# Layer 0's two ends: the first keys' logarithms by products on TensorE, split weights, and the last projection spread between the last attention's steps

## The chip, the cores and the metric

The kernel runs on one NeuronCore of a Trainium2 chip. The metric is the device time of one execution in microseconds (us), lower is better. The profile is one execution recorded by the hardware profiler; its span is a little shorter than the time of the same execution as a run.

## The reference, cut to what matters

The network has four layers on x of shape (2, 512, 32, 32): a deformable attention with an MLP (layer 0), and three more attention layers. Only layer 0's attention is touched by the change. All arithmetic is in 32-bit floats.

```python
xn  = bn(x);  q = gconv1x1(xn, qw)                      # 8 groups of 64 channels
off = gelu(depthwise 6x6, stride 4, of q + dw_b)        # 8x8 places per group
off = tanh(off_pw_w . off) * 4                          # 64 sampling places, the keys
kv  = grid_sample(xn, places);  k, v = gconv1x1(kv, kw), gconv1x1(kv, vw)
pos = grid_q - grid_kv                                  # 1024 queries x 64 keys x (x, y)
bias = sign(pos) * log1p(abs(pos))
bias = relu(bias @ cpb_w1 + cpb_b1)                     # 2 -> 128
bias = relu(bias @ cpb_w2 + cpb_b2)                     # 128 -> 128
bias = bias @ cpb_w3 + cpb_b3                           # 128 -> 1
attn = softmax(q.k * scale + bias);  out = attn @ v
x = x + out_w @ out + out_b                             # the projection, then the MLP
```

The position `pos` separates into an x part and a y part, so for each key only 32 logarithms in x and 32 in y are needed. The first of the three small layers is a sum of an x table and a y table; the second (128 by 128, for each of 1024 queries and 64 keys, in 16 groups) is the bulk of layer 0's work.

## The kernel before, in words

The 512 channels lie in four tiles of 128 partitions (`CT`), for each of the two images (`B`). Two groups share a tile of 128 channels, so there are eight pairs (`BP`) and sixteen units `u`, one for each image and group.

**The front of a pair** (`offsets`, then `sampled`). `offsets` scales x to `xn` (L230), multiplies by the q weights (L237, `l0qkv[:, 0]`), copies q into a padded tile (L240), multiplies six rows of taps on DVE (`prod`, L244), reduces them (`conv`, L257), and then goes through gelu (L260), two tiny products (L265), tanh (L267), and the positions (L269 to L272) to `log`, the logarithms: 128 keys on the partitions, 32 in x and 32 in y on each (L280 to L284). It writes `log` to DRAM (`logs`, L286), and the places (`spots`, L288). `sampled` reads the places back, transposes `xn` (L305), builds bilinear weights `w` (L308 and after), sums `kv` by 32 records of products (L332: for each of the two halves of the channels, eight blocks of 128 pixels), and forms k and v (L345 to L353). Both are generators: the first pair's `offsets` runs straight through at the start, later ones go a step at a time between other work.

**The bias.** `table` loads 16 keys' logarithms, spread to all 128 partitions, from the DRAM copy by a DMA on SP's queue (L365: `lb`), makes the x table on POOL (`tx`, L367), and the y table on DVE into the PSUM tile `bank` (L379). `first_hidden` adds x and y tables and clips at zero by a custom DVE instruction (`h`, L391). `second_hidden` multiplies by `l0w2`, 32 hidden units at a time with four keys side by side (`hp`, L422), evicts on ACT (L427), and adds up the four parts by ACT, POOL and accumulating DMAs (L414 to L440). For the last block these sums are on DVE (L412, L440). `last_product` (L454) puts the sums into `sim` in PSUM. `l0w2` is `cpb_w2` times the magnitudes of `cpb_w3`; that multiplication (L183, L184, on `w3row`) is in `last_weights`.

**The attention** (`attend`) adds q·k to `sim` (L469), copies to `ss` (L477), transposes (L481), takes the softmax (L486 to L493), transposes back (L497, L501), multiplies by v (L506) and copies to `att` (L509). Its PSUM tiles come from the pool `ps`, three buffers of two banks, shared with `hp`. `project` and `project_one` multiply `att` by `ow` (L524) and add to x on DVE (L528): for each of four output tiles and two halves of the pixels, four products. The second image's projection comes after the last attention. Then `mlp0` loads its weights on SP's queue (L542), scales x on DVE (L550) and multiplies (L558, L567).

**What sets the order.** Layer 0 is inside `manual_schedule` for PE, ACT, DVE and POOL: these engines run in the order in which the code is written. The loop over `quads` (16 units, 8 blocks of keys, 2 halves) keeps `first_hidden` one quad ahead of `second_hidden`, and steps one generator of `front` and one of `after` at each quad. DMAs on SP's queue, and the work of `mlp0`, are placed by the framework. The first loads are issued on ACT's queue in this order: `cols`, `grid`, `l0_qkv` (768 KB), `cpb_w2`, `out_w`, `cpb_w3`; x goes on SP's.

Of the kernel before, what the change touches and what calls it, by code (L numbers as in the profile page):

```python
# [18 lines left out]
P = 128  # L19
# [28 lines left out]
class Net:  # L48
# [16 lines left out]
    def prologue(self, ctx: ExitStack):  # L65
        nc, io = self.nc, self.io
        const = self.const = self.pool(ctx, "const")
        xpool = self.pool(ctx, "x")
        self.cols = const.tile([P, NCOL], F32, tag="cols", name="cols")
        nc.scalar.dma_start(self.cols, io["cols"])  # L70
        self.grid = const.tile([P, NGRID], F32, tag="grid", name="grid")
        nc.scalar.dma_start(self.grid, io["grid"])
# [26 lines left out]
    def layer0(self):  # L99
# [3 lines left out]
        with ExitStack() as ctx:  # L103
            keep = self.pool(ctx, "l0")
            self.l0qkv = keep.tile([P, 3, CT, P], F32, tag="qkv", name="qkv")
            nc.scalar.dma_start(self.l0qkv, io["l0_qkv"])
            self.l0w2 = keep.tile([P, P], F32, tag="w2", name="w2")
            nc.scalar.dma_start(self.l0w2, io["cpb_w2"])
            ow = keep.tile([P, CT, C], F32, tag="ow", name="ow")
            nc.scalar.dma_start(ow, io["out_w"])  # L110
            self.s1 = self.bn(keep, "bn1")
            self.last_weights(keep)
# [62 lines left out]
    def last_weights(self, keep):  # L175

# [1 line left out]


        nc = self.nc  # L180
        row = keep.tile([P, P], F32, tag="row", name="w3row")
        nc.scalar.dma_start(row, self.io["cpb_w3"].partition_broadcast(P))
        nc.vector.scalar_tensor_tensor(row, row, -1.0, row, ALU.mult, ALU.max)  # L183
        nc.vector.tensor_tensor(self.l0w2, self.l0w2, row, ALU.mult)  # L184
# [11 lines left out]
        for k in range(4):  # L196
            rows = slice(32 * k, 32 * k + 32)
            nc.vector.tensor_copy(self.ends[rows, 28 + k : 29 + k], sign[rows, 3:4])

    @staticmethod  # L200
    def step(behind):
# [21 lines left out]
    def offsets(self, m, bt, ps):  # L223
# [65 lines left out]
        m["logs"], m["spots"] = logs, spots  # L289
        yield  # L290

    def sampled(self, m, bt, ps):
# [33 lines left out]
        nc.vector.scalar_tensor_tensor(w, w, 0.0, wx.unsqueeze(1).to_broadcast([P, NB, 2 * NJ]), ALU.max, ALU.mult)  # L326
        yield
        kv_ps = self.bank[:, 384:448]
        for par in range(2):
            rows = slice(par * DH, (par + 1) * DH)  # L330
            for n in range(NB):
                nc.tensor.matmul(  # L332
                    kv_ps[rows, :],
                    lhsT=xnT[:, n, rows],
                    rhs=w[:, n, rows],
                    start=(n == 0),
                    stop=(n == NB - 1),
                )
# [18 lines left out]
    def table(self, u, o, pairs, tables):  # L357
# [9 lines left out]
            nc.gpsimd.tensor_scalar(x, got[:, :, :, 0, :], self.col("cpb_w1", 0), self.col("cpb_b1"), ALU.mult, ALU.add)  # L367
            tables["next"] = got, x

        if o % 2 == 0:  # L370
            if u == o == 0:
                load(0, 0)
            tables["logs"], tables["x"] = tables.pop("next")
        elif u < 2 * BP - 1 or o < 7:

            load(*((u, o // 2 + 1) if o < 7 else (u + 1, 0)))
        y = self.bank[:, 0:256].rearrange("p (j i x) -> p j i x", j=2, i=4)
        i = 4 * (o % 2)
        nc.vector.tensor_scalar(y, tables["logs"][:, :, i : i + 4, 1, :], self.col("cpb_w1", 1), None, ALU.mult)  # L379
# [82 lines left out]
    def attend(self, u, m, sim, att, ps):  # L462
# [16 lines left out]
        tp = ps.tile([P, 8, NJ], F32, tag="ps", name=f"tp{u}")  # L479
# [12 lines left out]
        nc.vector.reciprocal(st[:, 2, :], st[:, 1, :])  # L492
        nc.vector.tensor_tensor(e, e, st[:, 2, :].unsqueeze(2).to_broadcast([P, 8, NJ]), ALU.mult)  # L493
        yield
        pp = ps.tile([P, HF], F32, tag="ps", name=f"pp{u}")
        for i in range(4):
            nc.tensor.transpose(  # L497
                pp[:, i * P : (i + 1) * P], e[:, 2 * i : 2 * i + 2, :].rearrange("p a j -> p (a j)"), self.ident
# [1 line left out]
        pt = self.soft.tile([P, HF], F32, tag="pt", name=f"pt{u}")  # L500
        nc.vector.tensor_copy(pt, pp)  # L501
        yield
        o = ps.tile([P, N], F32, tag="ps", name=f"o{u}")
        for h in range(2):
            half = slice(h * NJ, (h + 1) * NJ)
            nc.tensor.matmul(  # L506
                o[rows, h * HF : (h + 1) * HF], lhsT=m["v"][half, rows], rhs=pt[half, :], start=True, stop=True
            )
        nc.scalar.copy(att[g // 2][rows, :], o[rows, :])  # L509
        yield  # L510

    def project(self, ps, att, w, bias: str, b: int):
# [652 lines left out]
```

## Time and profile before

| | |
|---|---|
| three timed runs | 3599.56, 3600.17, 3602.11 us; median 3600.17 |
| profiled execution | 3599.09 us as a run, span 3597.3 us |
| mean TensorE clock granted | 0.989 |
| PE busy, 0 to 42 us | 3.85 us |
| PE busy, 42 to 60 us | 17.76 of 18 us |
| PE busy, 60 to 2080 us (layer 0's loop) | 2007.84 of 2020 us |
| PE busy, 2080 to 2100 us (last attention) | 11.04 of 20 us |
| PE busy, 2100 to 2130 us (last projection) | 29.11 of 30 us |
| PE busy, 2130 to 3597 us (MLP, layers 1 to 3) | 1430.98 of 1467 us |

PE is TensorE's multiplication, PEld its weight loads, DVE is VectorE, ACT is ScalarE, POOL is GpSimd, SP the queue of SyncE. A 32-bit product is recorded as two rows ("x2" for one matmul). In the page, a group is line, engine, operation, output and inputs, count, then busy time and mean duration; behind the next bar stand the idle time of the engine just before and what ended it. In a timeline, a row is start, busy time, engine, line, what, and in brackets the idle time before. In the chain of waits, a row is start, length and what the end of the program waited for.

### The profile page before, as it was taken

Reading aid. Unit: us, or ns where it says so; the run is one execution under the profiler, and the core shown is the slowest. Engines: PE = TensorE matmul, PEld = TensorE weight load, DVE = VectorE, ACT = ScalarE, POOL = GpSimd, SP = SyncE. Lnnn points to the kernel's source line nnn. Section 1 sums busy time; section 2 is a strip of 40 time slices with the busy share of each in tenths; the row PEclk is TensorE's granted clock in tenths of the full one; section 3 lists DMA queues with packets and bytes.
Section 4 is the critical chain, followed back from the end, with each engine's and each line's share of the span. In section 5 each row is a group of like instructions: output and inputs, shape, how many; then the busy total and the mean of one; then the engine's idle time right before and its main releaser. Section 6 shows DMA issues by size and latency. Waiting matters only on the chain.

```text
span 3597.3 us, 58774 instructions
## 1 busy us (share of the span) xinstructions
PE 3500.6 (97%) x25152; PEld 1249.1 (35%) x25152; DVE 2019.9 (56%) x2074; ACT 1974.7 (55%) x2001; POOL 1871.8 (52%) x1393
## 2 busy tenths in 40 slices
PE   5999999999999999999999989999999999999999
PEld 2333332332333332332333334444644333443333
DVE  5767767767767668768666620000242476423664
ACT  4877777787776677777777720111010465102661
POOL 3878787787786687787788810000011344012441
PEclk8999999999999999999999999999999999999999
DMA  5878777787786687787788740000000000000001
GB/s 144 157 138 158 149 154 144 151 161 146 152 160 125 122 161 143 149 160 147 165 163 161 147 159 0 0 0 0 1 3 0 36 1 2 15 0 1 1 1 48
DMA packets 101924, 335.20 MB, mean 93 GB/s; under 512 B 12560, under 2 KB 14224, under 8 KB 100368
## 3 DMA queue, kind: packets, MB, share of 16 engines
q0 software_dynamic: 73296, 266.90, 39.2%
q1 hardware_dynamic: 27488, 62.34, 5.9%
q8 instruction: 201, 3.29, 0.4%
q10 hardware_dynamic: 864, 2.06, 0.2%
q14 instruction: 75, 0.61, 0.1%
HBM read 59.92 MB, written 4.46 MB: 18 GB/s over the span
## 4 chain that ended last, share of the span: by engine, by line
PE 93%; DVE 5%; DMA 1%; issue 0%; ACT 0%; POOL 0%; ACTq 0%; SPq 0%; DVEq 0%; POOLq 0%
PE hp L422 47%; PE m L558 6%; PE m L567 6%; PE o L924 6%; PE s L895 6%; PE pb L524 3%; PE qk0p L787 3%; PE qk1p L787 3%; PE sim L454 3%; PE vp L828 3%; PE out_b L524 2%; DVE h L391 2%; DVE prod L244 1%; PE d L941 1%; DVE conv L257 1%
## 5 line engine op out<-in xcount | busy, mean ns | idle before, releaser
L422 PE MATMUL hp<-h,w 128*32 128x512 f32 x16384 | 1823.4, 593 | 17.7 <-DVE h L391 16.2
L391 DVE CUSTOM_DVE_ANT_1 h<-tx,bank 128x1024 f32<-128x1024 f32 x1024 | 1181.0, 1216 | 345.0 <-PE hp L422 321.9
L427 ACT ACTIVATE h<-hp,magb 128x1024 f32<-128x1024 f32 x1024 | 1123.6, 1112 | 451.5 <-PE hp L422 450.6
L422 PEld LDWEIGHTS hp<-h,w 128*32 128x32 f32 x16384 | 528.9, 110 | 1242.3 <-issue 1152.5
L414 POOL DMA_DIRECT2D h<-h x509 | 452.3, 1026 | 377.1 <-ACT h L433 319.9
L440 POOL TENSOR_TENSOR h<-h,h 128x1024 f32<-128x1024 f32 x255 | 614.7, 2410 | 21.3
L438 POOL TENSOR_SCALAR h<-h,flip 128x1024 f32<-128x1024 f32 x256 | 449.0, 1754 | 0.9 <-ACT h L427 0.9
L899 ACT ACTIVATE e<-s 128x1024 f32<-128x1024 f32 x256 | 258.6, 1024 | 153.4 <-PE s L895 153.3
L429 ACT ACTIVATE h<-h,flip 128x1024 f32<-128x1024 f32 x256 | 291.3, 1138 | 0.0
L895 PE MATMUL s<-q,k 64*64 64x512 f32 x2048 | 260.0, 590 | 5.4 <-ACT e L899 3.7
L924 PE MATMUL o<-e,v 64*64 64x512 f32 x2048 | 260.8, 592 | 0.1
L598 POOL MEMSET l1ones<- 128x128 f32 x1 | 0.2, 205 | 486.4 <-PE m L567 486.4
L562 ACT ACTIVATE mh<-m,cols 128x512 f32<-128x512 f32 x64 | 44.0, 687 | 336.5 <-PE m L558 336.5
L558 PE MATMUL m<-mx,w 128*128 128x512 f32 x512 | 220.5, 592 | 0.9 <-issue 0.9
L567 PE MATMUL m<-mh,w 128*128 128x512 f32 x512 | 220.4, 592 | 0.0
L906 POOL TENSOR_TENSOR some<-some,e 128x1024 f32<-128x1024 f32 x64 | 151.4, 2365 | 82.5 <-ACT e L899 80.1
L575 DVE SCALAR_TENSOR_TENSOR x<-m,cols,x 128x512 f32<-128x512 f32 x16 | 12.0, 751 | 318.0 <-PE m L567 318.0
L431 POOL TENSOR_SCALAR h<-h,flip 128x1024 f32<-128x1024 f32 x128 | 156.0, 1219 | 64.5 <-ACT h L427 63.6
L904 POOL TENSOR_TENSOR some<-e,e 128x1024 f32<-128x1024 f32 x32 | 75.9, 2371 | 213.3 <-ACT q L933 129.2
L801 POOL TENSOR_TENSOR sq<-q 128x1024 f32<-128x1024 f32 x16 | 30.3, 1895 | 280.0 <-DVE q L795 280.0
L799 ACT ACTIVATE k<-qk1p,cols 128x512 f32<-128x512 f32 x32 | 22.0, 688 | 243.5 <-PE qk1p L787 243.5
L433 ACT ACTIVATE h<-h,flip 128x1024 f32<-128x1024 f32 x128 | 145.6, 1138 | 0.0
(185 smaller groups left out, 2710.5 us busy)
## 6 DMA issues: line engine op xcount, KB each, us to landing
h<-h POOLq DMA_DIRECT2D x509, 512.0 KB, 6.5
lb<-logs SPq DMA_DIRECT2D x64, 512.0 KB, 5.3
w<-in_mlp_w SPq DMA_DIRECT2D x8, 1024.0 KB, 12.0
qkv<-in_l_qkv SPq DMA_DIRECT2D x8, 768.0 KB, 6.4
x<-in_x SPq DMA_DIRECT2D x8, 512.0 KB, 7.8
out<-x SPq DMA_DIRECT2D x8, 512.0 KB, 2.6
proj<-in_l_proj SPq DMA_DIRECT2D x8, 256.0 KB, 5.9
l1w<-in_l_w SPq DMA_DIRECT2D x1, 1280.0 KB, 8.7
```

Of the source, the lines that this page charges most:

```text
L391: self.nc.vector._custom_dve(TENSOR_ADD_SAT, out=h[:, k, :, :], in0=x[:, jj, 2 * r + k, :].unsqueeze(1).to_broadcast([P, H, W]), in1=y[:, ...
L414: nc.gpsimd.dma_start(to, what, accum_op=ALU.add)
L422: nc.tensor.matmul(hp[rows, cut], lhsT=self.l0w2[:, 32 * q : 32 * q + 32], rhs=h1[k][:, cut], start=True, stop=True)
L427: nc.scalar.activation(y, hp, AF.Relu, bias=self.magb[:, q : q + 1])
L429: nc.scalar.activation(ys[0], ys[0], AF.Copy, scale=self.flip[:, 0:1])
L438: nc.gpsimd.tensor_scalar(y, y, self.flip[:, 2:3], 1.0, ALU.mult, ALU.mult)
L440: (nc.vector if final else nc.gpsimd).tensor_tensor(y, y, ys[2], ALU.add)
L558: nc.tensor.matmul(acc, lhsT=w1[t][:, o * P : (o + 1) * P], rhs=xn[t], start=(t == 0), stop=(t == CT - 1))
L567: nc.tensor.matmul(acc, lhsT=w2[t // 4][:, t % 4, o * P : (o + 1) * P], rhs=hs[t], start=(t == 0), stop=(t == nh - 1),)
L895: nc.tensor.matmul(s[halves[c], par, :], lhsT=ks[p][rows, at : at + DH], rhs=qs[p][rows, cut], start=True, stop=True)
L899: nc.scalar.activation(e, s, AF.Exp)
L924: nc.tensor.matmul(o[halves[par], r, :], lhsT=v[rows, n, at : at + DH], rhs=e[rows, par, :], start=(n == 0), stop=(n == NB - 1),)
```

## The change

1. The first load. `l0_qkv` is split: the q third (256 KB) goes second on ACT's queue, ahead of `grid`; the k and v thirds go after `cpb_w2` and `cpb_w3`, ahead of `out_w`.
2. `fold_weights`: the two DVE instructions that multiply `l0w2` by `w3row` move behind the first pair's `conv`.
3. The first 16 keys' logarithms are no longer loaded from DRAM. Sixteen products with a column of the identity matrix, repeated 128 times as weights, spread a row of `log` over all partitions into a PSUM tile (`lb_ps`). ACT makes the x table from it and copies it to `lb`; DVE takes the first y table from PSUM, the second from the copy. POOL's first `tx` and SP's first `lb` load are gone.
4. In `sampled`, the loops over channel halves (`par`) and pixel blocks (`n`) change places.
5. The end. `held` has the last two blocks' sums. The new generator `share` keeps three output tiles of the last projection in the three buffers of `ps`, and adds the products of one `att` tile at a time: `att[0]` between the two `last_product` calls, `att[1]` after the q·k step, `att[2]` after the softmax's first step, `att[3]`, with the additions to x, at the end. The last `attend` uses `bank` and `sim` for its PSUM tiles, and its last copy is split between ACT and DVE. The fourth output tile is projected last, as before.

```diff
-            nc.scalar.dma_start(self.l0qkv, io["l0_qkv"])
+            nc.scalar.dma_start(self.l0qkv[:, 0], io["l0_qkv"][:, 0])
+            nc.scalar.dma_start(self.grid, io["grid"])
...
+            nc.scalar.dma_start(self.l0qkv[:, 1:3], io["l0_qkv"][:, 1:3])
...
-                for _ in self.offsets(pairs[0], 0, ps):
-                    pass
+                for n, _ in enumerate(self.offsets(pairs[0], 0, ps)):
+                    if n == 4:
+                        self.fold_weights()
...
-                for done in held:
-                    self.last_product(*done, sims, ps_s)
-                after.append(self.attend(u, pairs[u // 2], sims.pop(u), att, ps))
                 self.advance(after, lambda: False)
-                self.project(ps, att, ow, "out_b", B - 1)
+                self.last_product(*held[0], sims, ps_s)
+                accs = [ps.tile([P, 2, HF], F32, tag="ps", name=f"ob{o}") for o in range(CT - 1)]
+                share = self.share(accs, att, ow)
+                next(share)
+                self.last_product(*held[1], sims, ps_s)
+                for n, _ in enumerate(self.attend(u, pairs[u // 2], sims.pop(u), att, None)):
+                    if n in (0, 1):
+                        next(share)
+                for _ in share:
+                    pass
+                for h in range(2):
+                    self.project_one(ps, att, ow, "out_b", B - 1, CT - 1, h)
+
+    def share(self, accs, att, w):
+        nc = self.nc
+        for t in range(CT):
+            for o, acc in enumerate(accs):
+                for h in range(2):
+                    nc.tensor.matmul(
+                        acc[:, h, :],
+                        lhsT=w[:, t, o * P : (o + 1) * P],
+                        rhs=att[t][:, h * HF : (h + 1) * HF],
+                        start=(t == 0),
+                        stop=(t == CT - 1),
+                    )
+                    if t == CT - 1:
+                        xt = self.xs[B - 1][o][:, h * HF : (h + 1) * HF]
+                        nc.vector.scalar_tensor_tensor(xt, acc[:, h, :], self.col("out_b", o), xt, ALU.add, ALU.add)
+            if t < CT - 1:
+                yield
...
-        for par in range(2):
-            rows = slice(par * DH, (par + 1) * DH)
-            for n in range(NB):
+        for n in range(NB):
+            for par in range(2):
+                rows = slice(par * DH, (par + 1) * DH)
...
+        if u == o == 0:
+            logs = self.ps_h.tile([P, 2, 8, 2, W], F32, tag="ps", name="lb_ps")
+            for j in range(2):
+                for k in range(8):
+                    key = j * 32 + k
+                    nc.tensor.matmul(
+                        logs[:, j, k, :, :].rearrange("p d x -> p (d x)"),
+                        lhsT=self.ident[:, key : key + 1].to_broadcast([P, P]),
+                        rhs=pairs[0]["log"].rearrange("p d x -> p (d x)"),
+                        start=True,
+                        stop=True,
+                    )
+            x = self.tab.tile([P, 2, 8, W], F32, tag="x", name="tx00")
+            nc.scalar.activation(
+                x, logs[:, :, :, 0, :], AF.Identity, scale=self.col("cpb_w1", 0), bias=self.col("cpb_b1")
+            )
+            got = self.lpool.tile([P, 2, 8, 2, W], F32, tag="logs", name="lb00")
+            nc.scalar.copy(got, logs)
+            tables["logs"], tables["x"], tables["rest"] = logs, x, got
...
-        o = ps.tile([P, N], F32, tag="ps", name=f"o{u}")
-        for h in range(2):
+        if ps:
+            o = ps.tile([P, N], F32, tag="ps", name=f"o{u}")
+            parts = [o[:, h * HF : (h + 1) * HF] for h in range(2)]
+        else:
+            parts = [self.bank, sim]
+        for h, part in enumerate(parts):
             half = slice(h * NJ, (h + 1) * NJ)
...
+        else:
+            nc.scalar.copy(to[rows, 0:HF], self.bank[rows, :])
+            nc.vector.tensor_copy(to[rows, HF:N], sim[rows, :])
```

More of the change, by code (lines that the diff above doesn't have):

```diff
@@ L71, in prologue @@
         self.grid = const.tile([P, NGRID], F32, tag="grid", name="grid")
-        nc.scalar.dma_start(self.grid, io["grid"])
         x_in = io["x"].rearrange("b (t p) h w -> b t p (h w)", p=P)
@@ L105, in layer0 @@
             self.l0qkv = keep.tile([P, 3, CT, P], F32, tag="qkv", name="qkv")
-            nc.scalar.dma_start(self.l0qkv, io["l0_qkv"])
+            nc.scalar.dma_start(self.l0qkv[:, 0], io["l0_qkv"][:, 0])
+            nc.scalar.dma_start(self.grid, io["grid"])
             self.l0w2 = keep.tile([P, P], F32, tag="w2", name="w2")
             nc.scalar.dma_start(self.l0w2, io["cpb_w2"])
+            self.s1 = self.bn(keep, "bn1")
+            self.last_weights(keep)
+            nc.scalar.dma_start(self.l0qkv[:, 1:3], io["l0_qkv"][:, 1:3])
             ow = keep.tile([P, CT, C], F32, tag="ow", name="ow")
             nc.scalar.dma_start(ow, io["out_w"])
-            self.s1 = self.bn(keep, "bn1")
-            self.last_weights(keep)
             self.dram = ctx.enter_context(self.tc.tile_pool(name="l0_d", bufs=2, space=bass.MemoryType.DRAM))
@@ L168, in layer0 @@
                 self.join(True)
-                for done in held:
-                    self.last_product(*done, sims, ps_s)
-                after.append(self.attend(u, pairs[u // 2], sims.pop(u), att, ps))
                 self.advance(after, lambda: False)
-                self.project(ps, att, ow, "out_b", B - 1)
+                self.last_product(*held[0], sims, ps_s)
[27 more added lines that the diff above has]
+                yield
     def last_weights(self, keep):
         nc = self.nc
[L181 to L184, printed above, removed]
+        self.w3row = keep.tile([P, P], F32, tag="row", name="w3row")
+        nc.scalar.dma_start(self.w3row, self.io["cpb_w3"].partition_broadcast(P))
         w3 = self.colr("w3r", 4)
@@ L198, in last_weights, with fold_weights @@
             nc.vector.tensor_copy(self.ends[rows, 28 + k : 29 + k], sign[rows, 3:4])
+    def fold_weights(self):
+        nc, row = self.nc, self.w3row
+        nc.vector.scalar_tensor_tensor(row, row, -1.0, row, ALU.mult, ALU.max)
+        nc.vector.tensor_tensor(self.l0w2, self.l0w2, row, ALU.mult)
     @staticmethod
@@ L288, in offsets @@
         nc.sync.dma_start(spots, at)
-        m["logs"], m["spots"] = logs, spots
+        m["log"], m["logs"], m["spots"] = log, logs, spots
         yield
@@ L368, in load @@
             tables["next"] = got, x
-        if o % 2 == 0:
-            if u == o == 0:
-                load(0, 0)
+        if u == o == 0:
[17 more added lines that the diff above has]
+            tables["logs"], tables["x"], tables["rest"] = logs, x, got
+        elif o % 2 == 0:
             tables["logs"], tables["x"] = tables.pop("next")
@@ L376, in table @@
             load(*((u, o // 2 + 1) if o < 7 else (u + 1, 0)))
+        if u == 0 and o == 1:
+            tables["logs"] = tables.pop("rest")
         y = self.bank[:, 0:256].rearrange("p (j i x) -> p j i x", j=2, i=4)
@@ L478, in attend @@
         yield
-        tp = ps.tile([P, 8, NJ], F32, tag="ps", name=f"tp{u}")
+        tp = ps.tile([P, 8, NJ], F32, tag="ps", name=f"tp{u}") if ps else self.bank.rearrange("p (a j) -> p a j", j=NJ)
         for i in range(4):
@@ L494, in attend @@
         yield
-        pp = ps.tile([P, HF], F32, tag="ps", name=f"pp{u}")
+        pp = ps.tile([P, HF], F32, tag="ps", name=f"pp{u}") if ps else self.bank
         for i in range(4):
@@ L502, in attend @@
         yield
-        o = ps.tile([P, N], F32, tag="ps", name=f"o{u}")
-        for h in range(2):
-            half = slice(h * NJ, (h + 1) * NJ)
[L506 to L509, printed above, removed]
+        if ps:
[4 more added lines that the diff above has]
+        for h, part in enumerate(parts):
+            half = slice(h * NJ, (h + 1) * NJ)
+            nc.tensor.matmul(part[rows, :], lhsT=m["v"][half, rows], rhs=pt[half, :], start=True, stop=True)
+        to = att[g // 2]
+        if ps:
+            nc.scalar.copy(to[rows, :], o[rows, :])
+        else:
+            nc.scalar.copy(to[rows, 0:HF], self.bank[rows, :])
+            nc.vector.tensor_copy(to[rows, HF:N], sim[rows, :])
         yield
```

## The prediction

> **What bounds the kernel now.** I read the page first: engine shares, then the 40 slices. TensorE is the bound almost everywhere; only a few slices show it idle, and the change touches two of them: the first slice, and the one around 2090 us that hides the end of layer 0.
>
> ```profile
> PE 3500.6 (97%) x25152; PEld 1249.1 (35%) x25152; DVE 2019.9 (56%) x2074; ACT 1974.7 (55%) x2001; POOL 1871.8 (52%) x1393
> ...
> PE   5999999999999999999999989999999999999999
> ```
>
> A microsecond saved where PE is full, or on a chain that PE waits for, is a microsecond of span; elsewhere nothing. So next the chain of waits over the first 60 us (start, length, what):
>
> ```profile
> 1.18 5.12 DMA grid<-in_grid
> 6.32 10.98 DMA w3row<-in_cpb_w
> 17.32 0.30 DVE w3row L183
> 17.64 0.04 DVE w L184
> 17.86 4.54 DVE prod L244 x6
> 22.42 4.01 DVE conv L257
> 31.11 3.74 DMA logs<-log
> 34.87 5.11 DMA lb<-logs
> 40.16 0.78 POOL tx L367
> 40.97 1.23 DVE h L391
> ```
>
> Until 42.24, when the first `hp` product starts, everything is latency. Two waits stand out: DVE is held for `w3row` until 17.3, though `qpad` was ready at 14.40; and `log`, finished at 30.37, goes to DRAM and back before the tables exist at about 40.0. The timeline adds the first product, held by its weights:
>
> ```profile
> 9.87 3.47 PE L237 MATMUL q<-xn,qkv 128*128 128x512 f32 x4 [9.87 <-DMA qkv<-in_l_qkv]
> ```
>
> `xn` ended at 6.99, so PE waited 2.9 us for the 768 KB load alone. The windows give PE 2007.84 busy of the 2020 us from 60 to 2080, so an earlier start is kept. Then the timeline at layer 0's end:
>
> ```profile
> 2084.80 1.07 PE L454 MATMUL sim<-h,ends 128*32 128x512 f32 x3 [2.38 <-DVE h L412]
> 2094.72 1.09 PE L497 MATMUL pp<-ident,e 128*128 128x128 f32 x4 [4.73 <-DVE e L493]
> 2098.59 29.36 PE L524 MATMUL out_b<-att,ow 128*128 128x512 f32 x64
> 2103.95 0.75 DVE L528 SCALAR_TENSOR_TENSOR x<-out_b,cols,x 128x512 f32<-128x512 f32 x1 [7.41 <-PE out_b L524]
> 2128.83 16.55 PE L558 MATMUL m<-mx,w 128*128 128x512 f32 x38 [0.89 <-issue]
> ```
>
> From about 2082 to 2098.6 PE has only the last attention's short products between DVE and ACT steps; then 64 records of projection, the first four at half speed, then the MLP. Last, groups by shape on PE (busy us, mean ns), for a part that the change's title does not name:
>
> ```profile
> L332 PE MATMUL bank<-w,xnT 128*64 128x64 f32 x256 | 16.6, 237 | 2.8 <-DVE h L391 2.8
> L661 PE MATMUL m<-kn,xT 128*128 128x65 f32 x128 | 14.6, 275 | 0.0
> ```
>
> **What the Trainium skill says.** "TensorE: Matmul & The Clock Gate", Part 1: PE runs at half clock after an idle window and at full clock after about 3.4 us of activity. The trace agrees: records start 0.86 us apart from 2098.6 to about 2101.7, 0.43 after; at 42 us the switch took about 4.7. The same page, "LDWEIGHTS (loading the stationary operand)": a load takes its columns over 1.2 GHz, 53 ns for 64. The trace agrees: 32 records of L332 take 1.76 us of loads, 55 ns each. "TensorEngine Tiling (Array Packing)", "Key Properties": different tiles can load and multiply in parallel. `hp` agrees: four 32-column loads of 0.11 us each together take 0.13. "PSUM — Partial Sum Buffer", the section on bank collisions: two engines must not touch one bank and quadrant at once, two reads included. The trace has such a wait: ACT's copy of `v` (L353) starts 0.03 after DVE's (L352) ends, both reading one `bank`.
>
> **The change, part by part.**
>
> *First weights.* The q third of `l0_qkv` (256 KB) is issued second on ACT's queue, ahead of `grid`; 768 KB landed at 9.8, having moved at some 219 KB/us (half of the 425 GB/s that the DMA view shows, the x loads taking the rest). 512 KB less is 2.3 us: landing 7.4, bounds 7.0 (then `xn` binds) and 8.6 (smaller packets, smaller share). Gain 2.4, from 1.3 to 2.9. The issues behind it (`grid`, w2, `w3row`, the other two thirds, `ow`, which now waits for x00 at about 6.2) leave ACT's queue by about 7, and its table load still ends before q's copy is due near 11. `grid`, w2 and `w3row` go early and small; they are needed from about 20. Two thirds of qkv and `ow` are needed only after 80 us.
>
> *The fold.* L183 and L184 go behind the reduce. DVE no longer waits 17.86 − 14.40 = 3.45 us; the 0.58 us of the two instructions lies under ge, its product and tanh (26.42 to 27.48, 1.06 us). Gain 3.45. Bounds 2.9 to 3.5.
>
> *Logs by products.* `log` would then end at 30.37 − 2.4 − 3.45 = 24.5. SP's DRAM write and the reload for later keys stay, off the path; one `lb` load leaves SP's queue, POOL's first tx (0.77) its own; the second `lb` load follows the DRAM write at about 29 and lands near 35, two table halves before its use. In their place: 16 products of 128x64, 32 records each with a 128-column load. L661 has just this form: 14.6/128 = 0.114 us each, load-bound, so 3.7 us at full clock, 7.3 at half. PE is cold; with 3.9 us at half clock (the middle of 3.1 and 4.7; about 17 records) and 15 after, 5.6 us, tail 0.3. Then ACT: tx from PSUM, 0.69 (as L562), the copy to `lb`, 1.02 (as L240), and only then DVE's y, 0.49: the built program has y wait for that copy, the collision rule. Hand-overs 0.2. So h begins at 24.5 + 5.9 + 0.7 + 1.0 + 0.5 + 0.2 = 32.8 instead of 40.97: 8.2 us for the three parts together. PE being warmed already may give 0.3 more (the first eviction came 2.64 us after the last h, about 2.0 when warm). Start: 8.5, bounds 6 (all cold, weights late) and 10.
>
> *kv products.* L332's two halves alternate now, so neighbours use different 64-column tiles. Each of 8 groups holds PE 1.82 us (82.80 to 84.62). If pairs run together, 16 × 0.055 + 0.15 = 1.05: 0.77 saved, 6 us over 8 groups; PE is full around them, ACT idles 2.8 us just after. No row shows two alternating 64-column tiles at K = 128, so the bounds are 0 and 7; I take 6, since `hp` alternates tiles at full overlap. The loss side is a rival below.
>
> *The end.* In before's clock. PE finishes the earlier held products' records near 2081.7 and starts six projection products (12 records, 5.15 us) on att0; the three PSUM buffers are free at 2081.14. Ends 2087.0. Then the last `sim` products and q·k, warm, 8 + 8 records four abreast: 1.7, to 2088.9. They were ready at 2084.8: the attention's chain is put back, and with it bn2s on DVE (queued ahead of ss), and SP's eight MLP loads, by 1.3 us. ss ends about 2090.1, hidden under att1's six products (to 2094.2), as are six mx on DVE. Transposes to 2094.9; max, subtract, exp, sum, reciprocal, multiply (0.68 + 0.69 + 0.63 + 0.68 + 0.19 + 0.69, hand-overs) to 2098.6, under att2's six (to 2099.8). Then bare again: pp, pt, o, copies to att3: to 2103.0. Last six on att3: the built program makes each second half wait for the DVE add of the first half of the same tile. Per tile: product to end 1.02, add 0.75, hand-overs 0.1, second half 0.86: 2.73, thrice 8.2, not 5.15. To 2111.2. Eight products of the fourth tile, 16 × 0.43 = 6.9, to 2118.0; drain, add: the MLP starts 2119.1 instead of 2128.83. Gain 9.8, bounds 8 (more drains between tile shapes) and 11.5 (no stall at the halves). The MLP's weights landed by about 2108; 1.3 later still leaves 9 us.
>
> Sum: 8.5 + 6 + 9.8 = 24.3 us against the profiled span 3597.3, which was 3599.09 as a run; the three timed runs lie from 3599.56 to 3602.11. From their median: 3600.17 − 24.3 = 3575.9.
>
> **Rivals.**
> 1. The alternation gives nothing, loads in both tiles sharing one path: 18.3 us, 3581.9. For: 55 ns is exactly one load's time. Against: four `hp` loads overlap. Chance 0.25.
> 2. One of the ends gives little: PE stays cold through the logs' products and the weights come late, and the share's inserted work drains PE at each change of shape: 6 + 8, with alternation 0 to 6: 14 to 20, so 3580 to 3586. Chance 0.12.
> 3. Slower: alternating 64-column tiles in L332 drains the array each time. A record then costs its latency, 0.222 us instead of 0.057: 32 × 0.222 − 1.82 = 5.3 more per group, 42 over 8, minus 18.3: 24 later, 3624. It cancels the rest from 0.071 us more per record. Against: `hp` changes tile at every record at 0.107. Chance 0.03.
> 4. The program doesn't do what it says: the end bound by something else (weights, a DVE queue), the start's gain lost again before 60 us: within 7 us of before. Chance 0.04.
> The likeliest, at 0.56, is the sum.
>
> **How the numbers follow.** 0.2% is 7.2 us, about what a measurement can tell from no change. Faster by over that: 0.56 + 0.25 + 0.12 = 0.93; same 0.04; slower 0.03. Range: best bounds 10 + 7 + 11.5 = 28.5 give 3571.7, the spread of runs 1 more: 3571; the upper end takes in rivals 1 and 2: 3587.
>
> **What would show it.** Right: `q` starts near 7.4, `prod` directly after q's copy, `lb_ps` 32 records in some 5.6 us, h before 33.5; L332 busy about 8 to 9 us instead of 16.6; MLP's first product 9 to 10 us earlier relative to the last `hp`; DVE adds between the halves in the att3 step. Wrong: PE waiting for `mlp_w` at the MLP's start; PE idle growing in 60 to 2080; L332 unchanged or longer; `hp` starting after 36.

## The result, and the profile after

The changed kernel takes 3578.0 us (median of six runs, 3576.96 to 3579.59) against 3601.1 (six runs beside them, 3597.06 to 3602.11): ratio 0.9938, interval 0.9925 to 0.9951. The forecast was 3575.9 in a range from 3571 to 3587. The profiled span falls from 3597.3 to 3576.3 us, by 21.0, where the sum said 24.3.

On the page, PE has almost the same busy time in a shorter span, the first slice is fuller, and the notch around 2090 us has closed:

```profile
PE 3497.6 (98%) x25184; PEld 1248.3 (35%) x25184; DVE 2023.0 (57%) x2075; ACT 1976.3 (55%) x2003; POOL 1869.8 (52%) x1392
...
PE   7999999999999999999999999999999999999998
```

The chain of waits at the start (start, length, what). Neither `w3row` nor a transfer of `log` stands in it any more:

```profile
6.04 0.82 DVE xn L264
...
6.91 3.79 PE q L271 x4
...
11.85 4.54 DVE prod L278 x6
...
24.14 0.24 DVE log L318
...
24.51 7.08 PE lb_ps L410 x32
...
32.39 0.91 ACT lb L422
...
33.33 0.50 DVE bank L433
33.85 1.23 DVE h L445
```

`q` no longer waits for its weights but for `xn`; `prod` begins 6.0 us earlier than before (11.85, not 17.86); the longest piece is now the 32 records of `lb_ps`. Between `lb` and `bank` is the wait that the prediction named: DVE's y table follows ACT's copy.

The kv products, a group by shape (busy us, mean ns, then the idle time before), formerly 16.6 and 237:

```profile
L366 PE MATMUL bank<-w,xnT 128*64 128x64 f32 x256 | 9.5, 229 | 2.8 <-DVE h L445 2.8
```

A single record is as long as before, but neighbours overlap: in seven of the eight groups 32 records take 1.15 us from the first start to the last end, formerly 1.90. And the end, in PE's timeline: the `att[3]` step with DVE additions between its halves, the fourth tile, the MLP:

```profile
2090.68 1.13 PE L193 MATMUL ob<-att,ow 128*128 128x512 f32 x2 [0.66 <-ACT att L569]
2092.65 1.98 PE L193 MATMUL ob<-att,ow 128*128 128x512 f32 x4 [0.84 <-DVE x L202]
...
2099.27 7.03 PE L585 MATMUL out_b<-att,ow 128*128 128x512 f32 x16
2107.19 1.10 PE L619 MATMUL m<-mx,w 128*128 128x512 f32 x2 [0.89 <-issue]
```

To see where the 21.0 us come from, I followed the same instruction through both timelines and took the difference of its starts, the lead:

| at | before, us | after, us | lead |
|---|---|---|---|
| first eviction of `hp` | 48.27 | 41.29 | 6.98 |
| last quad's `hp` | 2072.91 | 2061.67 | 11.24 |
| MLP's first product | 2128.83 | 2107.19 | 21.64 |
| end of the span | 3597.3 | 3576.3 | 21.0 |

In the loop the lead rises by some 0.75 us at each of the groups of kv products (0.5 at the second), about 5.8 in all, and it falls twice by about 0.8, near 612 and near 1116 us: 6.98 + 5.8 − 1.6 is 11.2. Both falls come at a front whose second step of three `prod` takes 6.06 us on DVE in the changed kernel and 5.28 in the kernel before. Below, the first is called the long way and the second the short way of this step. After the MLP's start 0.6 is lost again; nothing of the change lies there.

### The profile page after: what moved, and what is told of

Its sections match the earlier page's. It is cut to its first block, busy times and chain, and to the rows that moved or that the text cites. A ratio compares the mean times of both kernels' runs of the same rounds, so it can differ in the third digit from the quotient of the medians.

```text
span 3576.3 us, 58840 instructions
## 1 busy us (share of the span) xinstructions
PE 3497.6 (98%) x25184; PEld 1248.3 (35%) x25184; DVE 2023.0 (57%) x2075; ACT 1976.3 (55%) x2003; POOL 1869.8 (52%) x1392
## 4 chain that ended last, share of the span: by engine, by line
PE 94%; DVE 5%; issue 1%; ACT 0%; POOL 0%; DMA 0%; DVEq 0%; ACTq 0%
PE hp L476 47%; PE m L619 6%; PE m L628 6%; PE s L956 6%; PE o L985 6%; PE qk0p L848 3%; PE pb L585 3%; PE qk1p L848 3%; PE sim L508 3%; PE vp L889 3%; DVE h L445 2%; DVE prod L278 1%; PE out_b L585 1%; PE d L1002 1%; DVE conv L291 1%; PE ob L193 1%
## 5 line engine op out<-in xcount | busy, mean ns | idle before, releaser
L960 ACT ACTIVATE e<-s 128x1024 f32<-128x1024 f32 x256 | 258.7, 1024 | 152.7 <-PE s L956 152.6
```

The source lines that it names most:

```text
L960: nc.scalar.activation(e, s, AF.Exp)
```

## The experiments

Each kernel is the changed one with the edit shown, except where it says otherwise, and the times of before beside them were medians of 3600.0 to 3602.7 us. In the runs with extra products (e5, e8, e11, e12) nothing is left out; the extra results are read by nobody. What is compared is mostly a stretch of the profile. Each kernel left one profile, and its span also holds the losses of 0.8 us, whose number differs from one profile to the next.

**e1: the kv loops put back.**

```diff
-        for n in range(NB):
-            for par in range(2):
-                rows = slice(par * DH, (par + 1) * DH)
+        for par in range(2):
+            rows = slice(par * DH, (par + 1) * DH)
+            for n in range(NB):
```

> The changed kernel with the loops over channel halves and pixel blocks in the kv products put back. Theory (alternating 64-column tiles overlap, PE is the bound): the kv group is busy 16.6 us again instead of 9.5; each of the eight groups costs 0.75 us more, 6 us in all, and the two places where the changed kernel lost 0.8 us on DVE (near 612 and 1107 us in its trace) may fall either way: span 3576.3 + 4 to 6 = 3580 to 3582. Rival (the gain lies in the ends alone): within 1 us of 3576.3.

Measured: 3585.11 us, ratio 0.9952 (0.9935 to 0.9969), span 3579.6. The group is back where it was, with the alternation as the only difference:

```profile
L366 PE MATMUL bank<-w,xnT 128*64 128x64 f32 x256 | 16.6, 236 | 2.8 <-DVE h L445 2.8
```

The last `hp` starts at 2066.46 instead of 2061.67, 4.8 us later; with one more front that went the short way here (three, against two), that is 5.6 for the eight groups. The alternation is what saves the time in that group, and rivals 1 and 3 of the prediction are out.

**e2: the first keys from DRAM again.**

```diff
-        if u == o == 0:
-            logs = self.ps_h.tile([P, 2, 8, 2, W], F32, tag="ps", name="lb_ps")
...
-        elif o % 2 == 0:
+        if o % 2 == 0:
+            if u == o == 0:
+                load(0, 0)
...
```

> The changed kernel with the first 16 keys' logarithms loaded from DRAM again. Theory A (the products were worth little because PE was cold through all 32 records, 7.06 us): log still ends at 24.4, the reload takes the 10.6 us that it took in the kernel before, h starts at 35.0 instead of 33.85, span about 1.1 us longer, 3577.4. Rival B (the products made most of the start's 7 us): h near 39, span 3581.

Measured: 3581.03 us, ratio 0.9940 (0.9923 to 0.9956), span 3579.1. DVE's timeline, where h waits for the x table on POOL again:

```profile
35.67 9.14 DVE L425 CUSTOM_DVE_ANT_1 h<-tx,bank 128x1024 f32<-128x1024 f32 x8 [0.40 <-POOL tx L401]
```

`log` ends at 24.66 and h starts at 35.67, 11.0 us later. With the products it was 24.37 and 33.85, 9.5 us. The products are worth 1.5 us at h (1.9 at the first eviction, 43.52 against 41.29, less the 0.3 by which `log` was late), and not the 2.3 that their part of the sum contains (10.6 of before, from 30.37 to 40.97, less 8.3): the 7.06 us of `lb_ps` take most of what the two transfers took.

**e3: the end put back.** `share` is not used, and `attend` and `project` stand as before.

```diff
...
-                self.last_product(*held[0], sims, ps_s)
-                accs = [ps.tile([P, 2, HF], F32, tag="ps", name=f"ob{o}") for o in range(CT - 1)]
-                share = self.share(accs, att, ow)
...
+                self.project(ps, att, ow, "out_b", B - 1)
```

> The changed kernel with the end of layer 0 as it was: no share, the whole projection after the last attention. Theory: from the start of the last quad's hp to the MLP's first product 55.9 us again instead of 45.5, span 10.4 us longer, 3586.7. Rival (part of the gain at the end comes from the earlier MLP weights or from chance): under 8 us longer.

Measured: 3586.99 us, ratio 0.9955 (0.9939 to 0.9972), span 3586.5. PE's timeline, with the whole projection in one row again:

```profile
2061.80 7.05 PE L468 MATMUL hp<-h,w 128*32 128x512 f32 x64
...
2087.03 28.35 PE L577 MATMUL out_b<-att,ow 128*128 128x512 f32 x64
2116.27 4.10 PE L611 MATMUL m<-mx,w 128*128 128x512 f32 x9 [0.89 <-issue]
```

From the last quad's `hp` (2061.80) to the MLP (2116.27) it is 54.47 us, with the share 45.52, in the kernel before 55.92. So the share is worth 8.95 to 10.4. The two kernels without it differ by 1.4, of which 1.0 is in the projection itself: 28.35 us for its 64 records here, 29.36 before.

**e4: the two fold instructions back in front of `prod`.**

```diff
-                for n, _ in enumerate(self.offsets(pairs[0], 0, ps)):
-                    if n == 4:
-                        self.fold_weights()
+                for _ in self.offsets(pairs[0], 0, ps):
+                    pass
```

> The changed kernel with the two instructions that fold the last weights put back ahead of the first pair's prod, the order of the loads as changed. Theory A (what removed the wait is that w3row is now loaded ahead of the large loads: it lands at 9.1, before q's copy ends at 11.75): no change, prod still starts at 11.85, span 3576.3 within 1. Rival B (the place of the two instructions removed it, as the prediction put it): prod starts some 3 us later, span 3579.5.

Measured: 3577.57 us, ratio 0.9929 (0.9913 to 0.9946), span 3576.7. DVE's timeline:

```profile
11.72 4.54 DVE L278 TENSOR_TENSOR prod<-qpad,cols 128x384 f32<-128x384 f32 x6 [2.01 <-ACT qpad L274]
```

`prod` still waits for `qpad` alone, and starts no later than at 11.85. In the new order `w3row` is issued at 2.86 instead of 6.32 and lands at 9.1, before q's copy ends. With these loads the place of the fold is worth nothing. No run has the fold moved and the loads in the old order.

**e9: one load of 768 KB, but second on the queue.**

```diff
-            nc.scalar.dma_start(self.l0qkv[:, 0], io["l0_qkv"][:, 0])
+            nc.scalar.dma_start(self.l0qkv, io["l0_qkv"])
...
-            nc.scalar.dma_start(self.l0qkv[:, 1:3], io["l0_qkv"][:, 1:3])
```

> The changed kernel with the q, k and v weights in one load again, second on ScalarE's queue, ahead of grid; all else as changed. Theory, that the gain before prod comes from the smaller first load alone and not from the place of the fold: q starts near 9.9 us instead of 6.91, prod near 14.8, and the lead is kept by all that follows: span about 3579.3, 3 us above the changed kernel. Rival, that the order on the queue (weights ahead of grid) is enough by itself: q starts before 8 and the span stays at 3576, within 1 us and the spread that the prod steps give.

Measured: 3577.88 us, ratio 0.9941 (0.9926 to 0.9956), span 3573.8. The chain of waits:

```profile
1.17 7.00 DMA qkv<-in_l_qkv
...
8.31 3.77 PE q L270 x4
```

Neither 9.9 nor 6.91: of the 2.96 us that `q` gained, 1.56 come from the new order alone, 1.40 from the smaller load. The new order is more than the place ahead of `grid`: `ow`, 1024 KB, was issued at 2.67 before, right behind the weights of q, and is issued at 4.83 here, so it takes less from them. No run separates the two. The span is nevertheless 2.5 us shorter than that of the changed kernel. At the first eviction e9 is 0.94 us behind, and at the last `hp` it is 1.46 ahead (2060.21). Three more of its front steps went the short way, described above; 0.94 − 3 × 0.8 is −1.46. Of two versions that differ by a microsecond, the span of a single profile says nothing here.

**e5: TensorE warmed.** Nine products into an unused tile behind q, three behind the product on gelu.

```diff
+                    if n == 1:
+                        warm = ps.tile([P, HF], F32, tag="ps", name="warm")
...
+                    for _ in range({1: 9, 6: 3}.get(n, 0)):
+                        nc.tensor.matmul(warm, lhsT=self.ident, rhs=pairs[0]["xn"][:, 0:HF], start=True, stop=True)
```

> The changed kernel with twelve products of no use ahead of the logarithms' products (nine of xn with the identity after q, three after tanh's product; nobody reads them), so that PE runs warm by then. Theory A (the 32 records took 0.22 us each because PE was at half clock throughout): 0.114 each, 3.7 us with the tail 0.3 to 0.4, h starts about 30.4 to 30.7 instead of 33.85, the first hp products warm too, span 3.2 to 3.8 us shorter: 3572.5 to 3573. Rival B (such products with repeated weights are slow at any clock): lb_ps still 7 us, span unchanged or longer.

Measured: 3575.41 us, ratio 0.9929 (0.9914 to 0.9945), span 3573.1. The records of `lb_ps`, 7.08 us long in the chain of the changed kernel above, in e5's timeline of PE:

```profile
24.95 3.78 PE L414 MATMUL lb_ps<-log,ident 128*128 128x64 f32 x32 [0.42 <-DVE log L322]
```

7.06 is 0.22 a record, 3.78 is 0.118: the double and the single price of the row L661 that the prediction used. h starts at 31.02, 2.8 us earlier, although `log` ended 0.5 later. So the microsecond that the start lacks against the forecast (h at 33.85, not 32.8) is the half rate of these records. One part of the expectation did not come true: the first `hp` were not warm. PE sat idle for 3.65 us before them, and their groups of four records were 0.85 us apart again until about 37.1, then 0.43.

**e7: the y table ahead of the copy.**

```diff
-            nc.scalar.copy(got, logs)
...
+        if u == o == 0:
+            nc.scalar.copy(tables["rest"], tables["logs"])
```

> The changed kernel with ACT's copy of the spread logarithms placed after DVE's first y table. Theory (y waited for the copy, 0.9 us, because both read one PSUM tile): y starts right after tx, h at 32.95 instead of 33.85, span 0.9 us shorter. Rival (the copy then comes between later work and gives it back): h earlier by 0.9 but the first eviction unchanged, span unchanged.

Measured: 3578.13 us, ratio 0.9935 (0.9920 to 0.9951), span 3576.4. The y table starts 0.03 us after `tx` ends, at 32.62, and the copy waits for it in turn. h starts 8.81 us after `log`'s start, instead of 9.71: 0.9 us. At the first eviction, also counted from `log`'s start, 0.65 is left of it, 16.50 against 17.15. The wait was real; it is too small to be seen in the span.

**e6: in the `att[3]` step the halves outermost**, so that three products lie between the two halves of one tile.

```diff
-            for o, acc in enumerate(accs):
-                for h in range(2):
+            last = t == CT - 1
+            for o, h in [(o, h) for h in range(2) for o in range(CT - 1)] if last else [
+                (o, h) for o in range(CT - 1) for h in range(2)
+            ]:
+                acc = accs[o]
...
```

> The changed kernel with the last step of the share taking all three tiles' first halves, then all second halves. Theory (PE stalled three times for DVE's addition to the first half of the same tile): the step takes 5.2 to 5.4 us instead of 8.6, the MLP starts 3.2 us earlier, span 3573.1. Rival (the additions themselves, six of 0.75 us on DVE, set the pace): under 1 us.

Measured: 3574.43 us, ratio 0.9923 (0.9908 to 0.9939), span 3575.5. PE's timeline, without a wait for DVE between the halves:

```profile
2092.09 5.42 PE L196 MATMUL ob<-att,ow 128*128 128x512 f32 x12 [0.66 <-ACT att L572]
```

The fourth tile follows at 2097.34, 5.25 us after the step's start instead of 8.59, and from the last `hp` to the MLP it is 42.18 instead of 45.52: 3.3 us, the three stalls that the prediction had put into the step. The profiled span moved by 0.8 only: the last `hp` came 1.4 us later than in the changed kernel, as all six front steps took the long way here, and 1.1 was lost behind the MLP's start.

**e8: e5, e6 and e7 together.**

> The changed kernel with the twelve products of no use that warm PE, the halves outermost in the share's last step, and the copy after y. Theory: the three gains add, 3.5 + 3.2 + 0.9 = 7.6, span 3568.7, ratio to the kernel before about 0.992. Rival (the start's gain is lost again where DVE and POOL meet): 4 to 5 us, 3571.5 to 3572.5.

Measured: 3571.11 us, ratio 0.9915 (0.9901 to 0.9928), span 3569.6. h starts at 29.95; the MLP starts 6.2 us earlier than in the changed kernel (2101.03). That is 3.6 at the first eviction and 3.3 at the end, less 0.8 for one front step more that went the long way. In the span it is 6.7 of the 7.6 expected: the gains add, but for the copy's, of which e7 had already shown that part is gone at the first eviction.

**e10: VectorE's front steps cut finer.** A lead that falls inside the loop means that PE isn't as full there as its busy share says. Around five of the seven later `conv` (near 120 us there is no such loss, near 1110 only the first row), PE's timeline of the changed kernel looks like this:

```profile
353.37 9.77 PE L476 MATMUL hp<-h,w 128*32 128x512 f32 x63
...
363.85 8.49 PE L476 MATMUL hp<-h,w 128*32 128x512 f32 x62
```

64 records take 7.05 us when nothing holds them, and here 63 take 9.8 and 62 take 8.5, all of it "busy". On DVE the same stretch has no gap:

```profile
346.08 5.25 DVE L278 TENSOR_TENSOR prod<-qpad,cols 128x384 f32<-128x384 f32 x3
...
351.85 4.62 DVE L445 CUSTOM_DVE_ANT_1 h<-tx,bank 128x1024 f32<-128x1024 f32 x4
356.38 4.32 DVE L291 TENSOR_REDUCE conv<-prod 128x64 f32<-128x2304 f32 x1
360.62 4.61 DVE L445 CUSTOM_DVE_ANT_1 h<-tx,bank 128x1024 f32<-128x1024 f32 x4
```

The falls of the lead lie in the first row: 5.25 us is the short way, and near 597 us the same three `prod` take 6.06. Which way they go is seen on POOL in the changed kernel. The short way:

```profile
350.29 1.89 POOL L485 TENSOR_SCALAR h<-h,flip 128x1024 f32<-128x1024 f32 x1 [0.41 <-ACT h L481]
```

and the long way:

```profile
601.41 1.18 POOL L485 TENSOR_SCALAR h<-h,flip 128x1024 f32<-128x1024 f32 x1 [0.41 <-ACT h L481]
```

Where POOL's instruction is long, DVE's third `prod` is short, and the other way round. "SBUF — State Buffer", section "Who interferes with whom", of the Trainium skill says that DVE and GpSimd share a port pair under an exclusive lock; these rows agree with it, 0.8 us for the loser. Of the six later pairs that show it, four went the short way before, two after. The cut was meant to remove both losses:

```diff
-            if ky % 3 == 2:
+            if ky % 2 == 1:
...
-        nc.vector.tensor_reduce(conv, prod.rearrange("p a b j -> p j (a b)"), AX.X, ALU.add)
-        yield
+        for part in (slice(0, NJ // 2), slice(NJ // 2, NJ)):
+            nc.vector.tensor_reduce(
+                conv[:, part], prod.rearrange("p a b j -> p j (a b)")[:, part, :], AX.X, ALU.add
+            )
+            yield
...
```

(For the first pair the fold stays behind the whole of `conv`.)

> The changed kernel with VectorE's work of a front cut finer: the six prod instructions go two at a time over three quads instead of three at a time over two, and the conv reduce in two halves, one a quad. Theory, that a quad with 4.3 us of conv reduce and 4.6 us of h on VectorE takes 8.5 to 9.8 us where PE needs 7.05, and that three prods with an h do the same in a small way and meet POOL: the hp quads around each of the 7 later convs come back towards 7.05, 1 to 2.5 us saved per front, 12 us in all (6 to 20): span 3564, 3556 to 3570. Rival, that VectorE has no room in the neighbouring quads either, or that PE's records are full there whatever VectorE does: span within 3 us of 3576.3, with the same time moved to other quads.

Measured: 3600.46 us, ratio 1.0 (0.9991 to 1.0008), span 3600.1: 24 us worse than the changed kernel, outside both expectations. PE's waits in e10 from 60 to 2080 us (us in total, times, longest):

```profile
PE bank L369 <- DVE h L448: 25.0, 7, 4.8
```

In the changed kernel this wait is 2.8 us, once, as the end of the kv products' row above has it.

The two extra steps put every later step of the front two quads later, and there the weights `w` of the kv products come right behind `ss`, the start of `attend`'s softmax, on DVE. The h of that quad stands behind them, and PE's kv products wait for this h: 2.5 to 4.8 us in each of the seven later pairs. One such place in e10, on DVE:

```profile
441.07 0.75 DVE L534 TENSOR_SCALAR ss<-sim,cols 128x512 f32<-128x512 f32 x1 [4.01 <-PE sim L526]
...
442.44 2.42 DVE L361 TENSOR_SCALAR wx<-wx 128x128 f32<-128x128 f32 x1
...
447.25 4.61 DVE L448 CUSTOM_DVE_ANT_1 h<-tx,bank 128x1024 f32<-128x1024 f32 x4
```

The same place on POOL, then on PE:

```profile
442.41 2.37 POOL L497 TENSOR_TENSOR h<-h,h 128x1024 f32<-128x1024 f32 x1
...
451.92 1.15 PE L369 MATMUL bank<-w,xnT 128*64 128x64 f32 x32 [3.46 <-DVE h L448]
```

The softmax is the smaller part. `ss` takes 0.75 us, but the small instruction `wx`, which takes 0.23 where it stands in the changed kernel (422.48), takes 2.42 here: it begins with an addition on POOL and ends 0.08 us after it. The `wx` before it ends 0.08 us after another POOL instruction and takes 0.67 instead of 0.26. So 2.6 of the 3.5 us at this place are again DVE standing behind POOL, and the other five pairs whose wait is new show the same 2.42 or 2.43.

What the cut itself did stays visible. From the o product before `conv` to the product on gelu, four quads take 32.9 us here; two of the changed kernel and two undisturbed ones (19.9 + 14.6) take 34.5, so the cut gains 1.6 at this pair. The three `prod` steps last 1.7, 4.4 to 4.5 and 2.6 to 3.0 us in all six pairs, so the two ways are gone, though the sum, some 9.1, is no less than the 8.5 that two steps mostly take with the long way.

**e11: e8 and e10 together.**

> The changed kernel with everything together: the idle products ahead of the logarithms' products, the y table ahead of the copy, the halves outermost in the last att step, and VectorE's front steps cut finer. If the cut gives what the theory of the run before says, and the four are independent, it is the sum: 6.7 us for the first three (their run together measured a span of 3569.6) and 12 for the cut: span 3557.6 (3550 to 3564). If the cut gives nothing, the span is 3569 to 3571.

Measured: 3594.76 us, ratio 0.9983 (0.9976 to 0.9989), span 3594.5: 23.7 us of waits before the kv products again. The start lost too. PE's timeline:

```profile
21.53 5.49 PE L138 MATMUL warm<-xn,ident 128*128 128x512 f32 x6
```

In e5 these last three extra products took 2.84 us. In e11 PE reached the full rate earlier, at 10.7, so the nine before them ended at 18.6 already. After 2.6 us without work PE was at half rate again. The three held it so long that the first weight load of `lb_ps` came at 25.96, 1.2 us after `log` was ready (24.74), and h starts at 32.32 only.

**e12: e8, and only the conv cut, its second half in the quad of gelu**, so that all later steps stay in their quads. (For the first pair the fold moves one step later, behind the second half.)

```diff
+        for part in (slice(0, NJ // 2), slice(NJ // 2, NJ)):
+            nc.vector.tensor_reduce(
+                conv[:, part], prod.rearrange("p a b j -> p j (a b)")[:, part, :], AX.X, ALU.add
+            )
+            if part.start == 0:
+                yield
```

> The three edits of the run e8_all_three, and the conv reduce of each front in two halves of 2.2 us, the second in the quad of gelu, which follows it: unlike the cut of e10_split_steps, every later step of the front keeps its quad. Theory, that VectorE sets the pace where a whole conv (4.3 us) meets an h (4.6) in one quad, and that e10 lost its gain at kv because the weights w were moved two quads into the softmax: from the o product before a conv to the one on gelu behind it, two quads of hp take about 2 us less than in e8 in each of the 7 later pairs, no PE wait at kv; span 3569.6 - 14 = 3555.6, range 3553 to 3563. Rival, that the gain of the cut in e10 came from the prods in twos, not from the conv: these stretches last as in e8 and the span stays within 2 us of 3569.6.

Measured: 3567.12 us, ratio 0.9905 (0.9889 to 0.9922), span 3565.4, the fastest of all. PE's timeline in e8:

```profile
361.00 8.45 PE L484 MATMUL hp<-h,w 128*32 128x512 f32 x62
```

and in e12:

```profile
350.37 9.93 PE L488 MATMUL hp<-h,w 128*32 128x512 f32 x63 [0.57 <-DVE h L457]
...
361.00 7.45 PE L488 MATMUL hp<-h,w 128*32 128x512 f32 x61
```

Half of what I expected, 1.0 us, in the second quad, and in five of the seven pairs: near 120 and near 1110 us there was no second slow quad to shorten. The first, 9.93 us, is the same in both. The last `hp` starts 6.05 us earlier (2052.80 against 2058.85): five times 1.06, and 0.8 from one more short `prod` step. 1.85 were lost again behind the MLP's start, where the two kernels do the same. The first quad's 3 us remain; there the copy of `pt`, three `prod`, the y table and h stand one behind the other. PE waits before the kv products as in the changed kernel, 2.8 us, once. So `conv` can be cut with a gain when no later step moves, and e10 lost by what its added steps moved. No run has the cut of `prod` without an added step.

## Why the prediction was right, and where not

**q's weights.** The forecast was a landing at 7.4 and a gain of 2.4. They came in time for `xn`: start 6.91, gain 2.96, at the better end of the range given. The text credits the size of the load; e9 shows that about half comes from the order of the loads. That the landing was in time for `xn` is right, the price of the size alone was too high: 1.40 instead of 2.4.

**The fold, the step that failed.** "DVE no longer waits 17.86 − 14.40 = 3.45 us" is right, but the prediction booked it to the move of L183 and L184. e4 undoes the move and loses nothing: the reordered loads bring `w3row` by 9.1. I had written that `w3row` goes "early and small" and did not ask whether it would then still hold DVE. The sum was right all the same, since a wait can be gained once, whichever edit removes it. That the move alone would have removed it, with the old loads, is likely from the trace of before, but no run shows it.

**Logs by products, the term that was too small.** "3.9 us at half clock ... 5.6 us, tail 0.3" was 7.06. I let PE warm after a given time of work, and it stayed at half clock through all 32 records; e5 shows the other price, 3.78. tx at 0.78 instead of 0.69 and the other steps as priced put h at 33.85 instead of 32.8. Gain at h 7.1 instead of 8.2, and 7.0 at the first eviction, inside the bounds 6 to 10.

**kv products.** 6 us forecast, about 5.8 measured, and e1 gives the group's 16.6 back. The worked price, 1.05 us for a group instead of 1.82, was 1.15 instead of 1.90 in the trace.

**The end.** 9.8 forecast (its own times, 2128.83 − 2119.1, give 9.7), 10.4 measured against the kernel before, 8.95 against e3. The `att[3]` step took 8.59 instead of 8.2, its three stalls as described, and e6 removed them; it began 29.0 us after the last `hp` instead of 30.1.

**What the sum lacked.** 7.0 + 5.8 + 10.4 is 23.2. The profiled span shows 21.0, because two front steps went the long way on DVE (1.6) and 0.6 was lost behind the MLP's start. The two kernels' medians, over six runs each, differ by 23.1. That this comes nearer to 24.3 is in part luck: the profiled execution of before, 3599.09 us as a run, lay 2.0 below the median of its six. I had read 2007.84 busy of 2020 us as a sign that PE is full in the loop. e12 shows that part of this time is PE waiting for h with a record open, for a shorter step on DVE makes the "busy" time shorter. The change doesn't touch these waits, but the difference of 0.8 us from profile to profile and the next gain lie there.

Left open: what decides which of DVE and POOL goes first at the third `prod`, and why the time behind the MLP's start lies between 1467.6 us (e1) and 1470.4 (e12) in kernels that do the same there.

## What to carry to other kernels

When two edits remove the same wait, price the wait once and ask for each edit alone what would then end it. Price short products after an idle stretch at the cold rate throughout, unless something long has run just ahead of them; that is what this case showed. Filler products on an idle PE bought 2.8 us in e5, but they have to last until the work comes: in e11 they ended too early and then stood in its way. In an order written by hand, cutting a step in two moves all that follow: before adding a step, look at what its successors will meet on every engine, and keep the count of steps.

## What the runs showed of the hardware

- The half rate lasted through 7.06 us of back-to-back records with 64 columns, a weight load with each (0.22 us a record). The prediction quotes about 3.4 us from "TensorE: Matmul & The Clock Gate", Part 1; these rows don't agree with it. With 512 columns the time varied: q's products and the extra ones followed each other from 7.42 in e5, and weight loads went from 0.33 to 0.19 us at 13.4, 6.0 us later; the same row of products took 5.3 us to that point in e12 and 3.5 in e11, near the quoted figure.
- Gaps of at most 1.5 us in e5 left the full rate in place at `lb_ps` (0.118 us a record). After gaps of 1.8 us in e12 and 2.6 us in e11, weight loads were at 0.33 or 0.34 us again, in e12 1.8 us after the gap had ended (23.1).
- The trace's column of the granted clock reads 1.00 over `lb_ps` in the changed kernel, and in e5 on both sides of 13.4 us, so here it is no witness for the start; the rates above are read from the durations.
- Alternating between two 64-column tiles at 128 rows takes 32 records from 1.90 to 1.15 us.
- DVE and POOL, meeting in one stretch, cost one of the two about 0.8 us at the third `prod`: POOL's 1.18 became 1.89, or DVE's three `prod` 5.25 became 6.06. At `wx` in e10 it was DVE that lost 2.2 us, 0.23 became 2.42, to the end of a POOL instruction of 2.37.
- A busy share of 99% on PE hid 2.8 and 1.7 us of waiting (9.77 and 8.49 us against 6.94 and 6.83 at 7.05 for 64 records) in two quads around each of five `conv` of layer 0's loop.
